# A transpose moved from TensorE to 32x32 blocks on VectorE, another seven-product scheme for q, k and v, and another order in the last first-stage group

## The chip, the cores and the metric

The kernel runs on one core of a Trainium2 chip. The metric is the time of one launch on the device, in microseconds (us); lower is better. The engines are named as the profile names them: PE is TensorE, DVE is VectorE, ACT is ScalarE, POOL is GpSimd and SP is SyncE, which here only issues transfers.

## The reference

Two graph layers over 4096 nodes with 512 features and one adjacency matrix (4096 x 4096, ones with probability 1/128). Each layer's result is added to its input and normalised over the features.

```python
# layer 0: four heads of 128
support = x @ weight                       # (N, 4, 128) by heads
w = leaky_relu(f1[None] + f2[:, None], 0.2)   # f1, f2: support times weight_u, weight_v
attn = softmax(where(adj, w, -1e30)) * adj
x = layernorm(x + attn @ support + bias + x @ proj_w + proj_b)
# layer 1: eight heads of 64
q, k, v = x @ Wqs, x @ Wks, x @ Wvs
scores = q @ k.T / 8 + 0.01 * eye - 1e16 * (1 - max(adj, eye))
x = layernorm(x + concat_heads(softmax(scores) @ v) @ Wo)
```

## The kernel before

The program is one long sequence, written out by hand: the order of the Python statements is the order of each engine's queue. Work that is due some steps later is put in a list with `later.at(n, fn)` and issued by `later.step()`. The rows are taken in 8 groups of 512 (`G`, `NG`) or in 32 tiles of 128 (`P`, `NT`).

**First products (L847, to about 210 us).** For each group g, `x @ weight` (kind "s") and `x @ proj_w` (kind "b") are each made as seven block products with shared sums instead of eight. A group is thus 14 products; the list `usual` alternates the kinds, `begin` (group 0) takes all "s" first, and `end` (group 7) is an order of its own. Products 2, 3 and 4 accumulate onto the PSUM buffers of 1, 5 and 7 after ScalarE or VectorE has taken those out (L864 to L875). `dots` (L818, VectorE) makes f1 and f2 from the finished blocks; `factors` takes the exponentials on ScalarE, scales the values on GpSimd (L700) and stores them from SP. The rows of x arrive so that 32x32 block transposes on VectorE (`turn_x`, L741) give the layout that the products need. Before the first product 14 dummy transposes run on TensorE (L887). `early` starts the first aggregation steps (`signs`, `front`) within group 7.

**Aggregation (L1077, 210 to 1136 us).** Four windows w of 1024 target rows, four heads h, 32 source tiles j: 512 steps. In a step VectorE makes the weights p (L641; every second step also a masked sign, L636) three steps ahead (`LA`), in four buffers, and TensorE multiplies them with the values. `beside_unit` issues transfers beside the steps; u counts the steps of a window. At the end of a window the eight tiles are closed beside the next window's steps: `close` takes statistics on VectorE (L511, L513), `normalise` runs on ScalarE (L1050) and stores the row block to `x1_d`. Some steps later `turn` transposes the tile with four TensorE transposes into PSUM (L1058), and `turned` copies it out on ScalarE (L1063) and stores it to `x1T_d`. `load_xT` brings it back for the next stage.

**q, k and v (L1193 and L1186, to about 1438 us).** Four pairs of groups; for each pair, k, q and v are made by `gemm` as seven block products each. `order` is the order of the products, `of_weights` and `of_features` say which sums (L1157, L1161) they need, and `beside` hangs other work behind a product. Products 4, 5 and 7 accumulate onto the buffers of 2, 3 and 1. ScalarE copies (L1200), VectorE adds or copies (L1239, L1246, L1254) and GpSimd adds (L1215) put the results together, and SP stores them (L1206, L1211). The closing of window 3 runs beside the first sets of this stage. Three score tiles of the last stage are made before the last v product.

**Attention (L1128 and L1390, to the end).** 1024 units of scores, exponentials, mask and products with v, then the output projection. The change does not touch it, except for the shape of `x1_d`.

Of the kernel before, what the change touches and what calls it, by code (L numbers as in the profile page):

```python
# [429 lines left out]
def tile_gat_then_masked_attention(  # L430
# [59 lines left out]
    x1_d = [dram.tile([P, D], F32, name=f"x1_d{i}") for i in range(NT)]  # L490
# [6 lines left out]
    x1T_d = [dram.tile([P, KC, G], F32, name=f"x1T_d{g}") for g in range(NG)]  # L497
# [43 lines left out]
    def wait_by_tile(name, bufs, **kw):  # L541
# [16 lines left out]
    order = (2, 3, 4, 5, 1, 6, 7)  # L558
    of_weights = {1: ((0, 0), (1, 1), ALU.add), 2: ((1, 0), (1, 1), ALU.add),
                  5: ((0, 0), (0, 1), ALU.add), 6: ((1, 0), (0, 0), ALU.subtract),  # L560
                  7: ((0, 1), (1, 1), ALU.subtract)}
    of_features = {1: ((0, 0), (1, 1), ALU.add), 3: ((0, 1), (1, 1), ALU.subtract),
                   4: ((1, 0), (0, 0), ALU.subtract), 6: ((0, 0), (0, 1), ALU.add),
                   7: ((1, 0), (1, 1), ALU.add)}
    plain_weights = {3: (0, 0), 4: (1, 1)}
    plain_features = {2: (0, 0), 5: (1, 1)}
# [3 lines left out]
    with tc.tile_pool(name="l0", bufs=NG) as l0, \  # L570
# [75 lines left out]
        with tc.tile_pool(name="l0s", bufs=2) as sp:  # L646
# [76 lines left out]
            for c in range(NCJ):  # L723
# [4 lines left out]
                if c < NCJ - 3:  # L728
                    for k in range(CJ):
# [3 lines left out]
            early = {3: lambda: signs(0, 0, 0), 5: lambda: front(0, 0, 0), 6: lambda: front(0, 0, 1),  # L733
                     7: lambda: signs(0, 0, 2), 10: lambda: front(0, 0, 2)}
# [151 lines left out]
            for _ in range(14):  # L886
                nc.tensor.transpose(warm[:, 0:P], ident, ident)  # L887
# [15 lines left out]
            for m in range(2):  # L903
# [6 lines left out]
            end = [("s", 1), ("b", 1), ("s", 5), ("s", 2), ("s", 6), ("s", 7), ("b", 5),  # L910
                   ("s", 3), ("b", 2), ("s", 4), ("b", 6), ("b", 7), ("b", 3), ("b", 4)]
            for g in range(NG):
# [7 lines left out]
                for k, (kind, i) in enumerate(plan):  # L920
# [35 lines left out]
        xTs = {}  # L956
# [13 lines left out]
        with wait_by_tile("l0v", 2) as vp:  # L970
            pools[1] = vp, vp

            def beside_unit(w, h, j):
# [30 lines left out]
                elif u % 4 == 0 and NT <= u < NT + 4 * KC:  # L1004
# [578 lines left out]
```

## Time and profile before

| what | value |
|---|---|
| median of 3 runs | 3356.52 us (3354.63 to 3357.25) |
| profiled execution | 3352.42 us, span 3350.6 us |
| granted TensorE clock, mean | 0.998 |
| PE busy | 3321.0 us, 99% |
| DVE busy | 2361.2 us, 70% |
| ACT busy | 1987.3 us, 59% |
| POOL busy | 2222.0 us, 66% |
| aggregation products, L1077 | 919.2 us |
| q, k, v products, L1193 and L1186 | 298 us together |
| transposes of the first layer's result, L1058 | 128, of 273 ns |

The profile is of one execution, whose own time stands beside its span. Busy time of an engine is the union of its instructions; a matmul overlaps the next one's start, so what one costs is read from the distance of the starts. A row of the waits names who waited, for whom, the total in us, how often, and the longest. A row of the timeline has the start and the length in us, the engine, the line of the program, the operation and the tiles written and read.

### The profile page before, as it was taken

Reading aid. Unit: us, or ns where it says so; the run is one execution under the profiler, and the core shown is the slowest. Engines: PE = TensorE matmul, PEld = TensorE weight load, DVE = VectorE, ACT = ScalarE, POOL = GpSimd, SP = SyncE. Lnnn points to the kernel's source line nnn. Section 1 sums busy time; section 2 is a strip of 40 time slices with the busy share of each in tenths; the row PEclk is TensorE's granted clock in tenths of the full one; section 3 lists DMA queues with packets and bytes.
Section 4 is the critical chain, followed back from the end, with each engine's and each line's share of the span. In section 5 each row is a group of like instructions: output and inputs, shape, how many; then the busy total and the mean of one; then the engine's idle time right before and its main releaser. Section 6 shows DMA issues by size and latency. Waiting matters only on the chain.

```text
span 3350.6 us, 66620 instructions
## 1 busy us (share of the span) xinstructions
PE 3321.0 (99%) x27064; PEld 1947.6 (58%) x27064; DVE 2361.2 (70%) x2894; ACT 1987.3 (59%) x2463; POOL 2222.0 (66%) x1588
## 2 busy tenths in 40 slices
PE   9999999999999999999999999999999999999998
PEld 7889999999999755633333333333333333333332
DVE  6689898898999611167766667666666666667676
ACT  1366977878776421255656656566565656656564
POOL 5631040040020365589999999999999999999996
PEclk9999999999999999999999999999999999999999
DMA  8978969589531443379889987889989889897984
GB/s 189 231 182 155 242 153 209 140 194 189 149 105 64 118 159 113 138 206 209 197 206 219 223 208 188 212 195 246 207 193 211 193 204 253 190 210 186 212 195 112
DMA packets 399054, 620.41 MB, mean 185 GB/s; under 512 B 166672, under 2 KB 247568, under 8 KB 397712
## 3 DMA queue, kind: packets, MB, share of 16 engines
q0 software_dynamic: 97520, 258.77, 42.5%
q1 hardware_dynamic: 299344, 354.26, 34.4%
q8 instruction: 215, 3.52, 0.4%
q10 hardware_dynamic: 1872, 3.02, 0.3%
q14 instruction: 103, 0.84, 0.1%
HBM read 315.87 MB, written 117.64 MB: 129 GB/s over the span
## 4 chain that ended last, share of the span: by engine, by line
PE 87%; POOL 2%; DMA 2%; issue 1%; DVE 1%; ACT 0%; POOLq 0%; ACTq 0%; DVEq 0%
PE o_ps L1077 27%; PE o_ps L1390 24%; PE s_ps L1128 24%; PE s_ps L1193 5%; PE s_ps L1454 3%; PE s_ps L1186 3%; POOL q_sum L1365 2%; DMA p<-p 1%; PE s_ps L1409 0%; PE x_ps L1058 0%; POOL p L1375 0%; DMA k_d<-v_sb 0%; DVE p L1522 0%; PE x_ps L1186 0%; POOL q_sum L1361 0%
## 5 line engine op out<-in xcount | busy, mean ns | idle before, releaser
L1365 POOL TENSOR_TENSOR q_sum<-q_sum,p 128x1024 f32<-128x1024 f32 x538 | 1375.5, 2557 | 65.4 <-DMA p<-p 41.8
L1345 DVE TENSOR_TENSOR p<-s_ps,adjT 128x1024 f32<-128x1024 f32 x896 | 1043.6, 1215 | 467.9 <-ACT s_ps L1342 433.6
L1342 ACT ACTIVATE s_ps<-s_ps 128x1024 f32<-128x1024 f32 x1021 | 967.3, 1006 | 596.3 <-PE s_ps L1128 596.1
L1128 PE MATMUL s_ps<-q_sb,k_sb 64*64 64x512 f32 x8192 | 943.0, 589 | 1.8 <-DVE p L1345 1.8
L1390 PE MATMUL o_ps<-p,v_sb 64*64 64x512 f32 x8192 | 943.6, 590 | 0.0
L1077 PE MATMUL o_ps<-sup_t,p 128*128 128x129 f32 x8192 | 919.2, 275 | 1.2 <-DVE p L641 1.2
L1077 PEld LDWEIGHTS o_ps<-sup_t,p 128*128 128x128 f32 x8192 | 916.9, 192 | 1.4 <-DVE p L641 1.3
L641 DVE SCALAR_TENSOR_TENSOR p<-fr_t,dj,az 128x1024 f32<-128x1024 f32 x512 | 653.9, 1286 | 80.7 <-PE o_ps L1077 52.5
L1128 PEld LDWEIGHTS s_ps<-q_sb,k_sb 64*64 64x64 f32 x8192 | 312.5, 133 | 568.3 <-issue 454.5
L1390 PEld LDWEIGHTS o_ps<-p,v_sb 64*64 64x64 f32 x8192 | 310.1, 133 | 570.8 <-issue 560.8
L625 ACT ACTIVATE z<-fr_t,f 128x1024 fp8e4<-128x1024 f32 x512 | 558.2, 1144 | 124.1 <-DVE az L636 123.7
L1375 POOL DMA_DIRECT2D p<-p x412 | 438.9, 1305 | 10.2 <-PE o_ps L1390 8.6
L1041 POOL DMA_DIRECT2D agg<-base_d x32 | 28.7, 1208 | 516.0 <-ACT agg L1027 515.8
L1345 DVE TENSOR_TENSOR p<-s_ps,md 128x1024 f32<-128x1024 f32 x128 | 150.7, 1216 | 67.7 <-ACT s_ps L1342 63.4
L588 POOL COPY seen<-token 128x1 f32<-128x1 f32 x24 | 12.4, 516 | 248.4 <-DVE token L586 248.4
L636 DVE TENSOR_TENSOR az<-adjT,z 128x512 int32<-128x512 int32 x256 | 175.5, 686 | 2.0 <-ACT z L625 1.3
L1200 ACT ACTIVATE sb<-s_ps 128x1024 f32<-128x1024 f32 x35 | 35.9, 1025 | 192.6 <-PE s_ps L1193 129.8
L601 ACT ACTIVATE adjT<-stage 128x1024 fp8e4<-128x1024 bf16 x128 | 130.6, 1051 | 4.6 <-DMA stage<-adj_d 4.6
L1215 POOL TENSOR_TENSOR sb<-sb,sb 128x1024 f32<-128x1024 f32 x36 | 84.9, 2373 | 71.8 <-ACT sb L1200 71.8
L1239 DVE COPY k_sb<-s_ps 128x1024 f32<-128x1024 f32 x12 | 14.7, 1224 | 141.8 <-PE s_ps L1193 91.8
L1454 PE MATMUL s_ps<-wo_sb,on 128*128 128x512 f32 x240 | 110.8, 604 | 0.0
L1424 ACT ACTIVATE r<-r_h 32x256 f32<-32x256 f32 x248 | 102.3, 412 | 2.9
(179 smaller groups left out, 2134.5 us busy)
## 6 DMA issues: line engine op xcount, KB each, us to landing
p<-p POOLq DMA_DIRECT2D x412, 512.0 KB, 9.0
k_sb<-k_d SPq DMA_DIRECT2D x128, 512.0 KB
v_sb<-v_d SPq DMA_DIRECT2D x128, 512.0 KB
adj_d<-in_adj_dram POOLq DMA_DIRECT2D x32, 1024.0 KB, 10.7
sup_t<-sup_d SPq DMA_DIRECT2D x120, 258.0 KB
fr_t<-fr_d SPq DMA_DIRECT2D x16, 1024.0 KB
adjT_d<-adjT SPq DMA_DIRECT2D x32, 512.0 KB
adjT<-adjT_d SPq DMA_DIRECT2D x32, 512.0 KB
```

Of the source, the lines that this page charges most:

```text
L625: nc.scalar.activation(z[:, k, :], fr_t[w, h][:, 0, :], AF.Sign, bias=fs[j // GT][:, 0, (j + k) % GT, h:h + 1], saturate=False)
L636: nc.vector.tensor_tensor(az.bitcast(I32), adjT[w, j // CJ][:, j % CJ:j % CJ + 2, :].bitcast(I32), z.bitcast(I32), op=ALU.bitwise_and)
L641: nc.vector.scalar_tensor_tensor(p, fr[:, 1, :], dj[j // GT][:, j % GT, h:h + 1], az_t[w, h, j // 2][:, j % 2, :], op0=ALU.max, op1=ALU.mult)
L1077: nc.tensor.matmul(o[t // BK][:, t % BK, :], p[:, t * P:(t + 1) * P], s, start=(j == 0 and t % BK == 0), stop=(j == NT - 1), skip_group_ch ...
L1128: nc.tensor.matmul(s[c:c + MS, e, :], k[r, a + c:a + c + MS], qt[g, m][r, :], start=True, stop=True)
L1193: nc.tensor.matmul(half, a[:, c, n * P:(n + 1) * P], x[:, c, :], start=not more and c == 0, stop=c == 1, skip_group_check=True)
L1342: nc.scalar.activation(s, s, AF.Exp)
L1345: nc.vector.tensor_tensor(p, s, keep[:, None, :].to_broadcast([P, HP, G]), op=ALU.mult)
L1365: nc.gpsimd.tensor_tensor(q, q, p, op=ALU.add)
L1375: later.at(2, lambda: nc.gpsimd.dma_start(a, b, accum_op=ALU.add))
L1390: nc.tensor.matmul(o[c, n, :], v[r, j % CH, c], p[r, e, :], start=(j == 0), stop=(j == NT - 1))
L1454: nc.tensor.matmul(s, on_t[g][:, m, t * P:(t + 1) * P], wo_sb[:, m, :], start=(m == 0), stop=(m == NP1 - 1))
```

## The change

First, the first layer's result is no longer transposed on TensorE. `x1_d` now holds one array per group; `load_x1` reads half a group (256 rows) in four transfers so that each quarter of the partitions holds another 128 features, and `turn_x1` transposes it with one VectorE block transpose for each quarter of the result. The weights are loaded with their rows permuted to match, in four transfers where one was before (`load_w`). For the first pair of groups this is done beside the last window's steps; for a later pair it hangs beside the k and q products of the pair before. Second, q, k and v use another scheme of seven products, whose sums build on one another (the scheme of the first products). Feature sums of the later pairs move from GpSimd to VectorE, and in place of four GpSimd sums per set there is one. Third, the last group of the first stage takes all "s" products and then all "b" products, with `factors` after the eleventh product, and `early` is moved accordingly. Fourth, 46 dummy transposes run at the start in place of 14.

```diff
-    x1_d = [dram.tile([P, D], F32, name=f"x1_d{i}") for i in range(NT)]
+    x1_d = [dram.tile([G, D], F32, name=f"x1_d{g}") for g in range(NG)]
...
-    x1T_d = [dram.tile([P, KC, G], F32, name=f"x1T_d{g}") for g in range(NG)]
...
-    order = (2, 3, 4, 5, 1, 6, 7)
-    of_weights = {1: ((0, 0), (1, 1), ALU.add), 2: ((1, 0), (1, 1), ALU.add),
-                  5: ((0, 0), (0, 1), ALU.add), 6: ((1, 0), (0, 0), ALU.subtract),
-                  7: ((0, 1), (1, 1), ALU.subtract)}
-    of_features = {1: ((0, 0), (1, 1), ALU.add), 3: ((0, 1), (1, 1), ALU.subtract),
-                   4: ((1, 0), (0, 0), ALU.subtract), 6: ((0, 0), (0, 1), ALU.add),
-                   7: ((1, 0), (1, 1), ALU.add)}
-    plain_weights = {3: (0, 0), 4: (1, 1)}
-    plain_features = {2: (0, 0), 5: (1, 1)}
+    order = (1, 5, 2, 6, 7, 3, 4)
+    of_weights = {5: ((1, 0), (1, 1), ALU.add), 6: (5, (0, 0), ALU.subtract),
+                  7: ((0, 0), (1, 0), ALU.subtract), 3: ((0, 1), 6, ALU.subtract)}
+    of_features = {5: ((0, 1), (0, 0), ALU.subtract), 6: ((1, 1), 5, ALU.subtract),
+                   7: ((1, 1), (0, 1), ALU.subtract), 4: ((1, 0), 6, ALU.subtract)}
+    plain_weights = {1: (0, 0), 2: (0, 1), 4: (1, 1), 7: (1, 0)}
+    plain_features = {1: (0, 0), 2: (1, 0), 3: (1, 1)}
...
-            early = {3: lambda: signs(0, 0, 0), 5: lambda: front(0, 0, 0), 6: lambda: front(0, 0, 1),
-                     7: lambda: signs(0, 0, 2), 10: lambda: front(0, 0, 2)}
+            early = {5: lambda: signs(0, 0, 0), 8: lambda: front(0, 0, 0), 9: lambda: front(0, 0, 1),
+                     7: lambda: signs(0, 0, 2), 11: lambda: front(0, 0, 2)}
...
-            for _ in range(14):
+            for _ in range(46):
...
-            end = [("s", 1), ("b", 1), ("s", 5), ("s", 2), ("s", 6), ("s", 7), ("b", 5),
-                   ("s", 3), ("b", 2), ("s", 4), ("b", 6), ("b", 7), ("b", 3), ("b", 4)]
+            end = [(kind, i) for kind in ("s", "b") for i in (1, 5, 2, 6, 7, 3, 4)]
...
+                    if g == NG - 1 and k == 10:
+                        factors(g, s4)
...
                 if g + 1 < NG:
                     later.at(1, lambda g=g, s4=s4: factors(g, s4))
-                else:
-                    factors(g, s4)
...
-        def load_w(dst, src, c):
-            nc.sync.dma_start(dst[:, c], src[:, c * P:(c + 1) * P, :].rearrange("h p k -> p h k"))
-
-        def load_xT(g, pool=turn_p):
-            xTs[g] = pool.tile([P, KC, G], F32, name="xT1", bufs=2)
-            nc.sync.dma_start(xTs[g], x1T_d[g])
...
+        def load_w(dst, src, c, a):
+            f = a * P + c * SQ
+            nc.sync.dma_start(dst[a * SQ:(a + 1) * SQ, c],
+                              src[:, f:f + SQ, :].rearrange("h p k -> p h k"))
+
+        def load_x1(g, n, pool=turn_p):
...
+            if n == 0:
+                xTs[g] = pool.tile([P, KC, G], F32, name="xT1", bufs=2)
+            ys[g, n] = turn_p.tile([P, HG // SQ, P], F32, name="y1_sb", bufs=2)
+            for a in range(NQ):
+                nc.sync.dma_start(
+                    ys[g, n][a * SQ:(a + 1) * SQ],
+                    x1_d[g][n * HG:(n + 1) * HG, a * P:(a + 1) * P].rearrange(
+                        "(b r) f -> r b f", r=SQ))
+
+        def turn_x1(g, n, c):
+            nc.vector.transpose(
+                xTs[g][:, c, n * HG:(n + 1) * HG].rearrange("p (b r) -> p b r", r=SQ),
+                ys[g, n][:, :, c * SQ:(c + 1) * SQ])
...
-                elif u % 4 == 0 and NT <= u < NT + 4 * KC:
-                    load_w(wk, wks, (u - NT) // 4)
-                elif u == NT + 4 * KC + 16:
+                elif NT <= u < NT + KC * NQ:
+                    load_w(wk, wks, (u - NT) // NQ, (u - NT) % NQ)
+                elif u == NT + KC * NQ + CJ:
                     nc.vector.tensor_tensor(wk_low, block(wk, 1, 0), block(wk, 1, 1), op=ALU.add)
-                elif h == H0 - 1 and j in (NT // 2, NT // 2 + CJ):
-                    load_xT((j - NT // 2) // CJ)
+                elif u >= 2 * NT and u % CJ == 0:
+                    k = (u - 2 * NT) // CJ
+                    if k % 3 == 0 and k < 12:
+                        load_x1(k // 6, k // 3 % 2)
+                if w + 1 == NW and u >= 2 * NT + 8 and (u - 2 * NT - 8) % 3 == 0:
+                    k = (u - 2 * NT - 8) // 3
+                    if k < 16:
+                        turn_x1(k // 8, k // 4 % 2, k % 4)
...
-                    nc.sync.dma_start(x1_d[i], y)
+                    nc.sync.dma_start(x1_d[i // GT][i % GT * P:(i % GT + 1) * P, :], y)
                 later.at(6, normalise)
-                later.at(8 if w + 1 < NW else 11, lambda: turn(y, i))
-
-            def turn(y, i):
-                p = xp.tile([P, KC, P], F32, name="x_ps")
-                for c in range(KC):
-                    nc.tensor.transpose(p[:, c, :], y[:, c * P:(c + 1) * P], ident)
-                later.at(2, lambda: turned(p, i))
-
-            def turned(p, i):
-                x1T = turn_p.tile([P, KC, P], F32, name="x1T", bufs=4)
-                nc.scalar.activation(x1T, p, AF.Copy)
-                nc.sync.dma_start(x1T_d[i // GT][:, :, i % GT * P:(i % GT + 1) * P], x1T)
...
             for dst, src in ((wq, wqs), (wv, wvs)):
                 for c in range(KC):
-                    load_w(dst, src, c)
+                    for a in range(NQ):
+                        load_w(dst, src, c, a)
...
-                sb = {i: sp.tile([P, 2 * G], F32, name=f"sb{i}", bufs=1) for i in (2, 3, 1)}
+                u2, p5 = (sp.tile([P, 2 * G], F32, name=n, bufs=2) for n in ("u2", "p5"))
...
+                def add(dst, t):
+                    n = 2 * G // len(t)
+                    for k, src in enumerate(t):
+                        part = slice(k * n, (k + 1) * n)
+                        nc.vector.tensor_tensor(dst[:, part], src, u2[:, part], op=ALU.add)
+
                 t = {}
                 for i in order:
-                    if i in (2, 3) or i == 6:
+                    if i in (1, 5, 6):
                         t[i] = new()
-                    elif i == 1:
+                    elif i == 7:
                         t[i] = [xp.tile([P, GT, P], F32, name="x_ps").rearrange(
                             "p t r -> p (t r)") for _ in range(2)] if last else new()
                     else:
-                        t[i] = t[{4: 2, 5: 3, 7: 1}[i]]
-                    if i == 7 and last:
+                        t[i] = t[{2: 1, 3: 5, 4: 7}[i]]
+                    if i == 4 and last:
                         for n in range(3):
                             first[n] = score(0, 0, n)
                             nc.scalar.activation(first[n], first[n], AF.Exp)
-                    product(i, t[i], more=i in (4, 5, 7))
-                    if i in sb:
-                        copy(sb[i], t[i])
-                    if i == 3:
-                        pool(sb[3], sb[3], sb[2], ALU.subtract)
-                    elif i == 4:
+                    product(i, t[i], more=i in (2, 3, 4))
+                    if i == 1:
+                        copy(u2, t[i])
+                    elif i == 5:
+                        copy(p5, t[i])
+                    elif i == 2:
+                        copy(out["11"], t[i])
+                        store("11")
+                    elif i == 6:
+                        add(u2, t[i])
+                    elif i == 7:
+                        add(out["22"], t[i])
+                        pool(out["22"], out["22"], p5, ALU.add)
+                        later.at(1, lambda: store("22"))
+                    elif i == 3:
+                        add(out["12"], t[i])
+                        store("12")
+                    elif last:
                         copy(out["21"], t[i])
+                        pool(out["21"], out["21"], u2, ALU.add)
+                        store("21", nc.gpsimd)
+                    else:
+                        add(out["21"], t[i])
                         store("21")
-                    elif i == 5:
-                        nc.vector.tensor_copy(out["12"], t[i][0])
-                        store("12")
-                        pool(sb[2], out["21"], out["12"], ALU.subtract)
-                    elif i == 1:
-                        pool(sb[1], sb[1], sb[3], ALU.add)
-                        pool(sb[2], sb[2], sb[3], ALU.add)
-                    elif i == 6:
-                        nc.vector.tensor_tensor(out["22"], t[i][0], sb[1], op=ALU.add)
-                        store("22")
-                    elif i == 7:
-                        if last:
-                            copy(out["11"], t[i])
-                            pool(out["11"], out["11"], sb[2], ALU.add)
-                            store("11", nc.gpsimd)
-                        else:
-                            nc.vector.tensor_tensor(out["11"], t[i][0], sb[2], op=ALU.add)
-                            store("11")
                     for fn in beside.get(i, []):
                         fn()
                     later.step()
 
             for pair in range(NG // 2):
-                if pair + 1 < NG // 2:
-                    for n in range(2):
-                        load_xT(2 * (pair + 1) + n, turn_p if pair % 2 else sp)
+                more = pair + 1 < NG // 2
+                halves = [(2 * pair + 2 + n // 2, n % 2) for n in range(4)] if more else []
+
+                def bring(n):
+                    load_x1(*halves[n], turn_p if pair % 2 else sp)
+
+                def turn(n):
+                    for c in range(KC):
+                        turn_x1(*halves[n], c)
+
                 beside = {}
                 if pair == 0:
-                    combine_features(nc.vector, 0, 3)
-                    combine_features(nc.vector, 0, 4)
-                    for i in (5, 1, 6, 7):
-                        todo = beside.setdefault(order[order.index(i) - 3], [])
-                        todo.append(lambda i=i: combine_weights(nc.vector, wk, wk_s, i))
-                        if i != 5:
-                            todo.append(lambda i=i: combine_features(nc.vector, 0, i))
-                    beside.setdefault(1, []).append(
+                    combine_features(nc.vector, 0, 5)
+                    for n, i in ((1, 6), (5, 7), (2, 3)):
+                        beside.setdefault(n, []).append(
+                            lambda i=i: combine_weights(nc.vector, wk, wk_s, i))
+                    for n, i in ((1, 6), (5, 7), (2, 4)):
+                        beside.setdefault(n, []).append(
+                            lambda i=i: combine_features(nc.vector, 0, i))
+                    beside.setdefault(6, []).append(
                         lambda: nc.scalar.activation(wq, wq, AF.Copy, scale=float(KD) ** -0.5))
-                    for i, n in ((2, 1), (5, 6), (1, 6), (6, 7), (7, 7)):
+                    for i, n in ((5, 7), (6, 7), (7, 3), (3, 4)):
                         beside.setdefault(n, []).append(
                             lambda i=i: combine_weights(nc.gpsimd, wq, wq_s, i))
+                if more:
+                    for k, n in ((1, 0), (5, 1)):
+                        beside.setdefault(k, []).append(lambda n=n: bring(n))
+                    for k, n in ((7, 0), (4, 1)):
+                        beside.setdefault(k, []).append(lambda n=n: turn(n))
                 gemm(wk, wk_s, "k", pair, beside)
                 beside = {}
                 if pair == 0:
-                    for i in (2, 5, 1, 6, 7):
-                        beside.setdefault(i, []).append(
+                    for i, n in ((5, 5), (6, 2), (7, 6), (3, 7)):
+                        beside.setdefault(n, []).append(
                             lambda i=i: combine_weights(nc.gpsimd, wv, wv_s, i))
-                if pair == NG // 2 - 1:
+                if more:
+                    for k, n in ((1, 2), (5, 3)):
+                        beside.setdefault(k, []).append(lambda n=n: bring(n))
+                    for k, n in ((7, 2), (4, 3)):
+                        beside.setdefault(k, []).append(lambda n=n: turn(n))
+                else:
                     for c in range(3):
                         load_adjT(0, c)
                     load_q(0, 0)
                 gemm(wq, wq_s, "q", pair, beside)
                 beside = {}
-                if pair + 1 < NG // 2:
-                    for i in of_features:
-                        beside.setdefault(i, []).append(
-                            lambda i=i: combine_features(nc.gpsimd, pair + 1, i))
+                if more:
+                    for i, n in ((5, 5), (6, 6), (7, 7), (4, 4)):
+                        beside.setdefault(n, []).append(
+                            lambda i=i: combine_features(nc.vector, pair + 1, i))
                 else:
-                    beside[2] = [lambda: load_kv(0, 0, 0)]
-                    beside[3] = [lambda: [load_adjT(0, c) for c in range(3, NCJ - 2)],
+                    beside[5] = [lambda: load_kv(0, 0, 0)]
+                    beside[2] = [lambda: [load_adjT(0, c) for c in range(3, NCJ - 2)],
                                  lambda: [finish_md(0, t) for t in range(GT)]]
-                    beside[6] = [lambda: load_kv(0, 0, 1),
+                    beside[7] = [lambda: load_kv(0, 0, 1),
                                  lambda: [load_adjT(0, c) for c in range(NCJ - 2, NCJ)]]
                 gemm(wv, wv_s, "v", pair, beside)
                 xTs.pop(2 * pair)
...
```

More of the change, by code (lines that the diff above doesn't have):

```diff
@@ L955, in tile_gat_then_masked_attention @@
         wk_low = turn_p.tile([P, KC // 2, D // 2], F32, name="wk_low", bufs=1)
-        xTs = {}
-        def load_w(dst, src, c):
-            nc.sync.dma_start(dst[:, c], src[:, c * P:(c + 1) * P, :].rearrange("h p k -> p h k"))
-        def load_xT(g, pool=turn_p):
-            xTs[g] = pool.tile([P, KC, G], F32, name="xT1", bufs=2)
-            nc.sync.dma_start(xTs[g], x1T_d[g])
+        ys, xTs = {}, {}
+        def load_w(dst, src, c, a):
[15 more added lines that the diff above has]
+                ys[g, n][:, :, c * SQ:(c + 1) * SQ])
         def block(w, m, c):
@@ L1138, in tile_gat_then_masked_attention @@
                 for c in range(KC):
-                    load_w(dst, src, c)
+                    for a in range(NQ):
+                        load_w(dst, src, c, a)
             def spare():
                 return lp.tile([P, 2, 2, D // 2], F32, name="adjT1", bufs=NCJ + 3)
-            wk_s, wq_s = ([spare() for _ in range(3)] for _ in range(2))
-            wk_s, wq_s = ({i: t[n // 2][:, n % 2] for n, i in enumerate(of_weights)}
-                          for t in (wk_s, wq_s))
+            wk_s, wq_s = [spare()], [spare() for _ in range(2)]
+            wk_s = {5: wk_low, 6: wk_s[0][:, 0], 3: wk_s[0][:, 1], 7: block(wk, 1, 0)}
+            wq_s = {5: wq_s[0][:, 0], 6: wq_s[0][:, 1], 3: wq_s[1][:, 0], 7: block(wq, 1, 0)}
+            wv_s = {i: sp.tile([P, 2, D // 2], F32, name=f"wv_s{i}", bufs=1) for i in (5, 6, 3)}
+            wv_s[7] = block(wv, 1, 0)
             x_s = {i: spare().rearrange("p a b r -> p (a b r)").rearrange(
-                "p (c r) -> p c r", c=2) for i in (3, 4, 1, 6, 7)}
-            wv_s = {i: sp.tile([P, 2, D // 2], F32, name=f"wv_s{i}", bufs=1)
-                    for i in of_weights}
-            wk_s[2] = wk_low
+                "p (c r) -> p c r", c=2) for i in of_features}
             def features(pair, c, n):
@@ L1156, in combine_weights @@
                 a, c, op = of_weights[i]
-                engine.tensor_tensor(sums[i], block(w, *a), block(w, *c), op=op)
+                a, c = (sums[k] if isinstance(k, int) else block(w, *k) for k in (a, c))
+                engine.tensor_tensor(sums[i], a, c, op=op)
             def combine_features(engine, pair, i):
                 a, c, op = of_features[i]
-                engine.tensor_tensor(x_s[i], features(pair, *a), features(pair, *c), op=op)
+                a, c = (x_s[k] if isinstance(k, int) else features(pair, *k) for k in (a, c))
+                engine.tensor_tensor(x_s[i], a, c, op=op)
             def take_out(name):
@@ L1169, in gemm @@
                 out = {}
-                for n, c in enumerate(("21", "12", "22", "11")):
+                for n, c in enumerate(("11", "22", "12", "21")):
                     out[c] = take_out("k_sb" if n % 2 else "v_sb")
-                sb = {i: sp.tile([P, 2 * G], F32, name=f"sb{i}", bufs=1) for i in (2, 3, 1)}
+                u2, p5 = (sp.tile([P, 2 * G], F32, name=n, bufs=2) for n in ("u2", "p5"))
                 def new():
@@ L1458, in load_y @@
                 y_t[g, t] = wp.tile([P, D], F32, name="y1", bufs=5)
-                nc.sync.dma_start(y_t[g, t], x1_d[g * GT + t])
+                nc.sync.dma_start(y_t[g, t], x1_d[g][t * P:(t + 1) * P, :])
             def close1(g, t, s, wait=4):
```

## Prediction

> **What bounds the kernel now.** I read the page's busy line first, then the waits of TensorE, its groups by form, and its timeline where first-layer results are closed.
>
> ```profile
> PE 3321.0 (99%) x27064; PEld 1947.6 (58%) x27064; DVE 2361.2 (70%) x2894; ACT 1987.3 (59%) x2463; POOL 2222.0 (66%) x1588
> ```
>
> TensorE is busy for all but 29.6 us of 3350.6. A microsecond of its work that goes is a microsecond saved, provided that no other engine falls behind; everything that only moves work between the other engines is worth nothing while TensorE is fed. Its few waits:
>
> ```profile
> PE o_ps L847 <- DVE xT L741: 4.1, 1, 4.1
> PE o_ps L847 <- DVE base L870: 3.2, 2, 2.8
> ...
> PE o_ps L1077 <- DVE p L641: 1.2, 1, 1.2
> ...
> PE s_ps L1193 <- POOL adjT L1157: 0.7, 1, 0.7
> ```
>
> They lie at the start (8.7 us), at the seam from the first products to the aggregation (207.8 and 218.1), and at the first q product (1162.6). The work to be removed, by form:
>
> ```profile
> L1058 PE MATMUL x_ps<-ident,agg 128*128 128x128 f32 x128 | 19.2, 273 | 0.0
> ```
>
> 273 ns is the duration of one and 19.2 us their union with overlaps. What one displaces is read from starts in the timeline:
>
> ```profile
> 476.35 3.74 PE L1077 MATMUL o_ps<-sup_t,p 128*128 128x129 f32 x32
> 479.92 0.60 PE L1058 MATMUL x_ps<-ident,agg 128*128 128x128 f32 x4
> 480.36 1.95 PE L1077 MATMUL o_ps<-sup_t,p 128*128 128x129 f32 x16
> 482.14 0.60 PE L1058 MATMUL x_ps<-ident,agg 128*128 128x128 f32 x4
> 482.58 3.74 PE L1077 MATMUL o_ps<-sup_t,p 128*128 128x129 f32 x32
> ```
>
> Two aggregation steps take 3.57 us (1.785 each); the four transposes of a tile push the next start back by 0.44 us. VectorE in the same stretch:
>
> ```profile
> 480.57 0.69 DVE L511 BATCH_NORM_STATS2 bn_st<-agg 128x6 f32<-128x512 f32 x1
> 481.37 0.18 DVE L513 BATCH_NORM_AGGREGATE bn_mv<-bn_st 128x2 f32<-128x6 f32 x1
> 481.47 0.69 DVE L636 TENSOR_TENSOR az<-adjT,z 128x512 int32<-128x512 int32 x1
> ...
> 482.26 2.48 DVE L641 SCALAR_TENSOR_TENSOR p<-fr_t,dj,az 128x1024 f32<-128x1024 f32 x2
> ```
>
> It never waits there: 36.94 us busy in 458 to 497.
>
> **What the Trainium skill says.** "VectorE: DVE Perf Modes", The three transpose paths: VectorE transposes inside 32x32 blocks only. The trace agrees in that the existing transposes (L741) serve here only since the loads spread the rows over blocks; a 128x256 one takes 401 ns, and four start within 1.42 us, 0.355 apart. "TensorE: Matmul & The Clock Gate", PE-mode transpose: its output goes to PSUM and needs a copy afterwards. The trace shows that copy (ACT L1063, 0.58 us), which goes too. The same page, What's actually happening: TensorE runs at half clock until it has been busy for a window of some 3.4 us. The trace agrees: clock 0.51 in 8.4 to 11.8 us, after an idle 4.1 us. "GPSIMD Engine Reference", Specifications: GpSimd shares its SBUF interfaces with VectorE instructions of two SBUF inputs. Here two p steps that take 2.48 us alone took 3.19 at 194.85, while GpSimd added.
>
> **The parts and their costs.**
>
> *Transposes off TensorE.* 32 tiles x 0.44 us = 14.1 us removed: 24 tiles in the closing stretches of windows 0 to 2 (10.6), 8 in the q/k/v stage (3.5). The pitch there is the same (1179.91 to 1180.35).
>
> *What is late next.* In a closing stretch VectorE does eight pairs of normalisation statistics, some 0.80 us each, on top of 1.62 us per step (1.28 for p, half of 0.69 for the mask). It normally completes p 2.9 us ahead (p 14 at 461.8, used at 464.7) and regains about 0.15 us per step. The tightest is p 24: done at 483.5 (half of the last row above), used at 484.37, so 0.9 us are left. Four tiles' transposes precede it. Without them step 24 wants to start at 484.37 - 4 x 0.44 = 482.61, so TensorE waits 0.9 us. The other windows show the same pattern (715.7 against 714.8; 947.9 against 947.0). Cost 3 x 0.9 = 2.7 us. Bounds: 0, and 10.6 (all that was freed there).
>
> *Block transposes in window 3.* Sixteen of 0.36 us over 48 steps, 0.24 per two steps, beside a VectorE that waits 0.30 us for TensorE every two steps. Hidden; behind them queues p, with its 2.9 us lead. If the cover were gone, 5.7 us; below nothing is excluded, as TensorE waits for nothing there. I take 0. Their loads (SP, four of 128 KB per half) are issued some 8 steps (14 us) ahead; the nearest row, 256 KB of agg<-base_d, lands after 6.3 us.
>
> *q, k, v.* Still seven products of 3.44 us, so TensorE's work is equal. Per product set VectorE goes from three evacuations to four (4 x 1.22 = 4.9 us), plus eight block transposes (2.9) in k and q, or four feature sums (4 x 1.2) in v: at most 9.7 of 24.1 us. GpSimd drops from four sums of 2.35 us to one, and its five feature sums per pair go; ScalarE loses a copy. Hidden by 14 us of idle VectorE; without that cover 1 to 5 us per set. Product 2 adds onto the buffer of product 1 after a 1.02 us copy with product 5 (3.44) between, product 4 onto that of 7 with product 3 between: no wait. The q set's first product now takes an unsummed weight block, so the 0.7 us wait for L1157 goes. In the last v set the second early score needs the buffer of product 3, whose add (1.22 + 0.2) starts when only one score (0.9) lies between: + 0.5 us. Net -0.2, bounds -0.7 and +1.5.
>
> *Queues.* SP issues 64 block loads and 36 more weight loads, less 32 stores and 8 loads: + 60 of 0.4 to 0.7 us. wk's sixteen queue around a 3 MB load that ends by 975 and are used about 995. wq and wv (32 issues from 1127) end by 1149, and wq is scaled at about 1150, while TensorE needs it at 1161.7. ScalarE and VectorE work queued behind those waits is not due before then. Taken as 0; at worst 3.
>
> *Last group by kind.* VectorE ran without a pause from 191.26 (the sum after product 6) to p 4 at 217.9, and TensorE waited for it at 207.78 and 218.07. Ordered by kind, product 6 starts at 187.53 in place of 189.26, so this queue starts 1.73 us earlier with the same contents (both bias sums stay on VectorE). One gap of 0.5 us opens (product 3 ends at 192.9). Against that, GpSimd's value sums, which stretched VectorE's rows there by some 3.7 us, fall earlier, beside PSUM reads. b 4 then starts at about 204.8 without its wait, step 0 at 206.5, and step 4 follows p 4. Gain 1.3 to 3.7; I take 2.3, with 0 and 4 as bounds. Moving the factors to k = 10 puts two reductions and a small transpose (0.4 us) ahead of two adds: counted. GpSimd's sums, SP's four stores of values and four row stores come earlier; nothing in the first pass needs them before step 28.
>
> *Warm-up.* 32 more transposes. At the cold pitch (0.215) until the clock rises at about 5.0, then 0.11, they end at about 8.3, before xT at 8.67. Product 1 then runs at full clock and ends at 10.5 in place of 12.2. But its copy cannot start: ScalarE issues loads until 11.24 and loads a table until 12.54. So 0. Bounds: -1, and + 2.6 if the clock stayed low (46 x 0.215 + 3.56 ends at 14.8).
>
> Sum: -14.1 + 2.7 - 0.2 - 2.3 = -13.9 us. The profiled execution took 3352.4 us (span 3350.6), giving 3338.5; it lies 4.1 below the median of 3356.5, and against that the forecast is 3342.6.
>
> **Rivals.**
>
> *VectorE becomes the bound in the closing stretches.* For it: 95% busy there. Against: its lead is not used up before p 24. If all 10.6 us come back as waits for p, -3.5 - 0.2 - 2.3 = -6.0: 3350.5, no measurable difference.
>
> *The block loads land late (slower).* VectorE works in order, so a block transpose that waits for its load holds back the adds that free PSUM, and TensorE stops at the next product. Place: twelve half-loads in the q/k/v stage, rows of 512 bytes, the first behind 32 weight loads. Each is issued four or five products ahead (13.8 us or more), and 3.4 us more pass before the buffer is wanted. To end 6.7 us slower it takes 20.6 us of stalls, 1.7 per half: landing after 18.9 us, three times the 6.3 of the nearest row. Price at 20 us each: 12 x 2.8 = 33.6, so 3376.
>
> *The seam gives nothing and the start loses.* If contention moves with the sums and the clock stays low: -13.9 + 2.3 + 2.6 = -9.0: 3347.5. This is also the case that the reordering and warm-up don't do what they say.
>
> **How the numbers follow.** A measurement of this kernel tells about 0.2% (6.7 us) from no change. Forecast, gains of 10 to 18: 0.62. Seam and start lost, or more waits in closing, gains of 6.7 to 10: 0.17. VectorE bound: 0.11. Late loads: 0.10. Faster 0.79, same 0.11, slower 0.10. The range is 3336 (seam at 4, no closing waits: -13.9 - 1.7 - 2.7 = -18.3, and run to run 2) to 3351 (the VectorE case); beyond lie the late loads and half of that case.
>
> **What would show it.** No L1058 and no L1063; about 0.9 us of TensorE waits for p L641 in each of the three closing stretches; SP landing without VectorE waits on y1_sb; step 0 near 206.5; TensorE busy near 3307. Many TensorE waits behind transposes waiting for a DMA in 1140 to 1430, or a q/k/v stage longer than 298 us, would make it wrong.

## The result, and the profile after

The changed kernel takes 3376.6 us (median of 7 runs) where the kernel before takes 3353.9 beside it: a ratio of 1.0069, 95% interval 1.0058 to 1.0080. It is slower by some 23 us; forecast was a gain of 14. One of the seven executions took 9023 us, which nothing here explains; it is left out of the ratio. The other six lie between 3367.8 and 3388.6, a spread of 21 us where the seven of the kernel before have 4.8: what costs the time does not cost the same in each execution. The profiled execution took 3376.4 us.

The page's busy line of the kernel after:

```profile
PE 3320.9 (98%) x26968; PEld 1945.3 (58%) x26968; DVE 2402.3 (71%) x2981; ACT 1957.6 (58%) x2418; POOL 2098.6 (62%) x1535
```

TensorE issues 96 transposes less on balance (128 gone, 32 more in the warm-up) and yet is as long busy as before, and the span is 24 us longer. The waits of the kernel after (who waits for whom: us in total, times, longest):

```profile
ACT adjT L598 <- DMA stage<-adj_d: 60.4, 9, 12.1
PE o_ps L1083 <- DVE p L638: 25.5, 12, 5.0
PE s_ps L1201 <- POOL bn_nb L518: 4.8, 1, 4.8
PE o_ps L844 <- ACT z L861: 3.3, 1, 3.3
```

The last row lies at the start, at the second product. (Line numbers moved: p L641 is now L638, the aggregation L1077 is L1083, q/k/v L1193 is L1201.) The first row was 4.6 us before, the second 1.2. Where the time sits shows when the aggregation is cut into its 16 passes of 32 steps (four to a window, the very last left out), from the starts of its products. The last column is the time from the first product of the q/k/v stage to the first product with v in the stage behind it:

| us | window 0 | window 1 | window 2 | window 3 | q/k/v stage |
|---|---|---|---|---|---|
| before | 58.6, 57.2, 57.2, 57.2 | 60.7, 57.2, 57.2, 57.2 | 60.7, 57.2, 57.2, 57.2 | 60.7, 57.2, 57.2 | 299.2 |
| after | 58.8, 57.2, 57.2, 57.2 | 58.3, **61.3, 70.7**, 57.2 | 58.3, **62.7, 65.1**, 57.2 | 58.2, 57.2, 57.2 | 302.0 |

The first pass of each window, in which the tiles are closed, gained what was forecast. What was not forecast are 31 us in the passes behind it, in windows 1 and 2 alone. Some 22 us of it are waiting (25.5 in TensorE's row for p, less 3.7 that are left in version e5 below); the rest is TensorE at a lower clock after the waits (0.91 in 560 to 616 us, 1.00 in the 350 us ahead of that). One such stop in the timeline, on three engines:

```profile
808.92 2.00 ACT L598 ACTIVATE adjT<-stage 128x1024 fp8e4<-128x1024 bf16 x2 [5.79 <-DMA stage<-adj_d]
813.04 0.69 DVE L633 TENSOR_TENSOR az<-adjT,z 128x512 int32<-128x512 int32 x1 [3.44 <-ACT z L622]
815.17 6.19 PE L1083 MATMUL o_ps<-sup_t,p 128*128 128x129 f32 x53 [1.28 <-DVE p L638]
```

ScalarE takes its instructions in the order of its queue. It stops at the shrink (L598), since the data for it have not come. The shrink makes the next window's adjacency ready and is not urgent; the signs z queued behind it are, and the wait runs on through VectorE to TensorE.

The data come in two transfers. `narrow` (issued by GpSimd, L586; L589 before) rewrites 1 MB of the adjacency into `adj_d`; some steps later `turn_in0` (issued by SP, L592; L595 before) brings it in as a DMA transpose. The rows of both, taken by tile between 430 and 900 us (in the first line how long SP's queue was held by one transpose, as ns min/median/max; the second line is the narrowing transfer). Before:

```profile
L595 SPq DMA_TRANSPOSE stage<-adj_d x16: 4060/8276/14874, 512.5 to 860.5; - x16
DMA to landing us min/median/max: 8.5/13.3/23.5
```

After:

```profile
L592 SPq DMA_TRANSPOSE stage<-adj_d x16: 4042/8086/26212, 501.0 to 886.0; - x16
DMA to landing us min/median/max: 8.7/23.3/32.7
```

Neither was changed. The longest transpose took 26 us in place of 15, and the narrowing 23 in place of 13 in the median: they run at the same time. The DMA queues of the kernel after in such a stretch (757 to 783 us; packets, MB, share of 16 engines' time; q1 has SP's transfers, q0 GpSimd's):

```profile
q1 hardware_dynamic: 3990, 1.11, 82.8%
q0 software_dynamic: 1756, 1.76, 49.3%
```

82.8% of 16 x 26 us over 3990 packets is 86 ns a packet (the two shares add up to more than 100%, so packets of one queue overlap with those of the other, and the time of a packet holds waiting). Version e5 below has a transpose nearly alone (770 to 775 us):

```profile
q1 hardware_dynamic: 4128, 1.05, 95.4%
q0 software_dynamic: 26, 0.03, 15.3%
```

That is 18 ns a packet. The Trainium skill ("DMA: Bandwidth & Descriptors", Queues, rings and completion order) says that each DMA engine takes turns between the queues that have work for it, and sends a whole packet of one before it turns to the next. The traces agree in that SP's small packets suffer beside GpSimd's larger ones, by 4.7 times; that the turns are the reason is not shown, as a packet of the page holds several descriptors and need not be a packet of the profile. The same page (Rules for kernel authors), in a row on transfers that corrupt each other's data, says "A transpose next to ordinary DMAs needs nothing"; of time it does not speak, and time is what was lost here.

Why do they meet now? SP's queue in the closing of window 1 and 2 has the stores of the closed tiles, then the next values and factors, then the transposes. Window 2 before:

```profile
728.69 2.24 SPq L616 DMA_DIRECT2D fr_t<-fr_d  x1
731.02 13.17 SPq L988 DMA_DIRECT2D sup_t<-sup_d  x8
744.53 36.18 SPq L595 DMA_TRANSPOSE stage<-adj_d  x3
```

and after:

```profile
740.21 0.37 SPq L613 DMA_DIRECT2D fr_t<-fr_d  x1
740.68 8.18 SPq L1000 DMA_DIRECT2D sup_t<-sup_d  x8
749.56 69.04 SPq L592 DMA_TRANSPOSE stage<-adj_d  x3
```

From the start of the window (671.9 and 685.5) the transposes are issued at 72.6 before and at 64.0 after: SP gets through sooner without the x1T stores and what paced them (e2, e6 and e7 below). The narrowing is paced by VectorE's steps and hardly moved (its fourth transfer is issued at 69.9 and 68.7). By the packets' own times the first transpose starts 3.6 us after the fourth narrowing transfer before, and 1.9 us ahead of it after.

The second loss is at the start of the q set. The chain of work that ended last in 1140 to 1200 us, in order of time, names it from end to end:

```profile
1159.39 9.24 DMA wo_sb<-in_L_gnn_Wo_dram
1168.64 0.31 SPq L956
...
1169.60 7.60 DMA wq<-in_L_gnn_Wqs_dram
...
1183.98 0.46 SPq L967
...
1185.46 3.21 DMA y_sb<-x_d
...
1188.80 1.49 DVE xT L973 x4
```

and the timeline its price (TensorE's rows, and one of VectorE's):

```profile
1184.02 3.60 PE L1201 MATMUL s_ps<-xT,wq 128*128 128x512 f32 x8
1191.06 1.23 DVE L1229 TENSOR_TENSOR v_sb<-s_ps,u 128x1024 f32<-128x1024 f32 x1
1192.43 5.88 PE L1201 MATMUL s_ps<-adjT,adjT 128*128 128x512 f32 x8 [4.82 <-POOL bn_nb L518]
1198.15 3.60 PE L1201 MATMUL s_ps<-xT,wq 128*128 128x512 f32 x8
```

The ninth of 32 weight loads waits for `wo_sb`'s load from another engine to land, the block loads (y_sb, L967) follow the last of the 32, VectorE waits 10.2 us for them at its first block transposes, and TensorE stops for 4.8 us; its next product takes 2.3 us longer at the lower clock (0.61 in 1192.4 to 1198.2): 7.1 in all. The row names GpSimd's bn_nb, which this product doesn't read. VectorE's add behind the block transposes (L1229), which frees a PSUM buffer, ended at 1192.29: 0.14 us ahead of the product.

### The profile page after: what moved, and what is told of

It is laid out like the page before. It is cut to its first block, busy times and chain, and to the rows that moved or that the text cites. A ratio compares the mean times of both kernels' runs of the same rounds, so it can differ in the third digit from the quotient of the medians.

```text
span 3374.5 us, 66468 instructions
## 1 busy us (share of the span) xinstructions
PE 3320.9 (98%) x26968; PEld 1945.3 (58%) x26968; DVE 2402.3 (71%) x2981; ACT 1957.6 (58%) x2418; POOL 2098.6 (62%) x1535
## 4 chain that ended last, share of the span: by engine, by line
PE 71%; DMA 3%; DVE 1%; SPq 1%; ACT 0%; issue 0%; POOL 0%; POOLq 0%; DVEq 0%; ACTq 0%
PE o_ps L1419 26%; PE s_ps L1134 26%; PE o_ps L1083 8%; PE s_ps L1201 5%; PE s_ps L1483 3%; PE s_ps L1194 3%; DMA stage<-adj_d 2%; SPq L592 1%; PE s_ps L1438 1%; DVE p L638 0%; DMA p<-p 0%; DMA wo_sb<-in_L_gnn_Wo_dram 0%; DMA sup_t<-sup_d 0%; DVE p L1551 0%; DVE bn_st L510 0%; DMA wq<-in_L_gnn_Wqs_dram 0%
## 5 line engine op out<-in xcount | busy, mean ns | idle before, releaser
L1083 PE MATMUL o_ps<-sup_t,p 128*128 128x129 f32 x8192 | 924.8, 276 | 26.3 <-DVE p L638 25.5
L1083 PEld LDWEIGHTS o_ps<-sup_t,p 128*128 128x128 f32 x8192 | 922.0, 193 | 29.1 <-DVE p L638 28.1
L638 DVE SCALAR_TENSOR_TENSOR p<-fr_t,dj,az 128x1024 f32<-128x1024 f32 x512 | 648.3, 1284 | 59.6 <-PE o_ps L1083 32.5
L1404 POOL DMA_DIRECT2D p<-p x412 | 436.8, 1296 | 10.2 <-PE o_ps L1419 9.3
L1374 DVE TENSOR_TENSOR p<-s_ps,md 128x1024 f32<-128x1024 f32 x128 | 150.7, 1217 | 68.7 <-ACT s_ps L1371 64.5
L598 ACT ACTIVATE adjT<-stage 128x1024 fp8e4<-128x1024 bf16 x128 | 130.5, 1050 | 60.4 <-DMA stage<-adj_d 60.4
L1223 POOL TENSOR_TENSOR k_sb<-k_sb,p 128x1024 f32<-128x1024 f32 x12 | 30.8, 2564 | 196.7 <-DVE k_sb L1229 190.2
L1208 ACT ACTIVATE u<-s_ps 128x1024 f32<-128x1024 f32 x12 | 12.3, 1024 | 167.6 <-PE s_ps L1201 104.4
L1229 DVE TENSOR_TENSOR u<-s_ps,u 128x1024 f32<-128x1024 f32 x12 | 14.7, 1225 | 111.6 <-PE s_ps L1201 81.8
```

The source lines that it names most:

```text
L638: nc.vector.scalar_tensor_tensor(p, fr[:, 1, :], dj[j // GT][:, j % GT, h:h + 1], az_t[w, h, j // 2][:, j % 2, :], op0=ALU.max, op1=ALU.mult)
L1083: nc.tensor.matmul(o[t // BK][:, t % BK, :], p[:, t * P:(t + 1) * P], s, start=(j == 0 and t % BK == 0), stop=(j == NT - 1), skip_group_ch ...
L1374: nc.vector.tensor_tensor(p, s, keep[:, None, :].to_broadcast([P, HP, G]), op=ALU.mult)
L1404: later.at(2, lambda: nc.gpsimd.dma_start(a, b, accum_op=ALU.add))
```

## The experiments

Times are medians of the runs; the kernel before had 3354.5 to 3355.1 beside them. Waits and passes are those of the one profiled execution of each version.

**e1: the narrowing half a period earlier.**

```diff
-                        if u == (16 + 8 * c if w else 22 + 7 * c):
+                        if u == (12 + 8 * c if w else 22 + 7 * c):
```

> The changed kernel, with the transfers that narrow the next window's adjacency (windows 1 to 3) started four steps, 7.1 us or half of their period, earlier; the tokens on VectorE that release them move along. Nothing on TensorE changes. Theory A (collision: the DMA transposes of the next window's adjacency run while these transfers run, each slows the other, ScalarE waits at the shrink L598, and TensorE behind it): the transposes of window 3 sum to about 60 us in place of 94, ScalarE's waits at L598 for the stage fall from 60 us to under 10, the second and third passes of windows 1 and 2 go back to 57.2 us (from 61.3, 70.7, 62.7 and 65.1), and the time falls by about 31 us to 3343 to 3350. Rival B (VectorE's closing work is what delays p, whatever the transfers do): the passes stay above 61 us and the time stays at 3368 to 3389. Rival C (the SP queue is too full with the block loads of weights): as B, since the SP queue is unchanged.

3348.6 us, 0.9980 of before (0.9971 to 0.9989). All passes of windows 1 and 2 are 58.3 or 57.2, and ScalarE no longer waits for the stage there (one wait of 2.1 us is left, in window 0, whose narrowing was not moved). The twelve runs lie within 6.0 us of each other. By tile:

```profile
L592 SPq DMA_TRANSPOSE stage<-adj_d x16: 3883/4248/14689, 501.8 to 854.2; - x16
DMA to landing us min/median/max: 8.1/10.4/13.9
```

Both medians are now below those of the kernel before. Nothing was moved but the narrowing and VectorE's small token that releases it, so the collision is shown to be the cause of the 31 us (28.0 between the medians). The q/k/v stage kept its 302.1.

**e2: the traffic of the stores alone.** After the store of the row block:

```diff
+                if w + 1 < NW:
+                    later.at(10, lambda: nc.sync.dma_start(
+                        again_d[i // GT][:, :, i % GT * P:(i % GT + 1) * P],
+                        y.rearrange("p (c r) -> p c r", c=KC)))
```

> The changed kernel plus one store of each closed tile of windows 0 to 2 from SP, in pieces of 512 bytes, to an array that nothing reads. It brings back the traffic of the transposed store that the change took out, not the TensorE transposes. Theory A with its trigger (without these stores the transposes start some 5 us earlier against the narrowing transfers, and fall on top of them): the transposes of windows 2 and 3 go back to some 62 us each, the stalls of 31 us vanish, and the time is 3343 to 3350 although there is more to store. Rival: if the trigger is something else (the time that TensorE gained in the closing, or the added weight loads), more traffic changes nothing or makes it worse: 3368 to 3395.

3372.7 us (four runs, 3367.8 to 3387.7): the rival was right that this isn't enough. ScalarE's wait for the stage fell only to 37.2 us, from 60.4.

**e3: the kernel before with its narrowing half a period later** (20 + 8 * c in the same line).

> The kernel before, with the narrowing transfers of windows 1 to 3 started four steps (7.1 us, half of their period) later, nothing else. Theory A: the DMA transposes of the kernel before run between these transfers by luck of phase; shifted, they overlap for most of their length, the transposes of windows 2 and 3 sum to over 85 us each (62 and 59 now), ScalarE waits at the shrink for tens of us, and the kernel is slower than before by 10 to 35 us without any part of the change. Rival: if the stalls of the changed kernel come from its own new work, this stays within 4 us of 3354.

The median, 3357.0 us, would by itself fit the rival. But the 20 runs lie between 3352.4 and 3383.8, 8 of them above 3364, where the kernel before spans 3351.7 to 3358.4. The profiled one (3376.3) has a pass of 76.9 us in window 2 and none in window 1. So the kernel before has the same trap, and a shift in time alone sets it off; it is entered in some executions only, which I had not expected.

**e4: the load of wo_sb placed in the text behind the 32 weight loads.**

> The changed kernel, with the load of the output weights (wo_sb, from ScalarE's queue) placed in the program after the 32 loads of wq and wv. Theory: a transfer waits for the one eight places before it in the program, and so the ninth load of wq waits 14.5 us for wo_sb, and 11 us pass with an idle SP queue; moved, SP's wait for wo_sb goes, ScalarE's wait of 7.4 us before the scaling of wq goes, and with it TensorE's wait of 4.8 us at the third q product. The time falls by about 5 us (less than one run tells). Rival (GpSimd's own work, the statistics of the closing, delays the sum of wq): the 4.8 us stay.

A single run: 3390.4 us, SP's wait 15.6 and TensorE's 5.0 us. Neither went; the longer total is the collision again, which cost 43 us in the passes of this execution. The load's place in the text was not the place that it got among the transfers: by the trace it still increments the semaphore (100) that the ninth weight load waits for and increments next. The test needs a load that comes later in time.

**e5: e1, and wo_sb loaded at the second pair of groups.**

```diff
-        nc.scalar.dma_start(wo_sb, wo.rearrange("(c a) k e -> (a k) c e", a=HP))
...
+                if pair == 1:
+                    nc.scalar.dma_start(wo_sb, wo.rearrange("(c a) k e -> (a k) c e", a=HP))
```

> The changed kernel with the narrowing transfers of windows 1 to 3 four steps earlier, and with the load of the output weights (wo_sb) issued at the start of the second pair of groups in the q/k/v stage, after all loads of wq and wv have landed. Moving that load behind the weight loads in the text of the program left SP's wait of 15 us as it was, since both became ready at the same place; here it cannot come between them. Theory (the ninth load of wq waits for wo_sb's to land, the scaling of wq, the sums on GpSimd and the first block transposes on VectorE are late by that, and TensorE stops 4.9 us and then runs its next product 2.3 us slower at a lower clock): SP's wait for wo_sb goes, the q set has no wait and all its products take 3.60 us, the q/k/v stage falls from 302.1 to about 295 us, and the time from 3348.6 by 7 to 3338 to 3345. Rival (the 32 weight loads themselves are what is late: GpSimd's and VectorE's waits stay): the stage stays at 302 us and the time at 3346 to 3351.

3341.1 us, 0.9960 of before (0.9946 to 0.9973): faster than both kernels. The stage takes 294.7 us, and the product that stopped runs without a wait:

```profile
1154.56 3.60 PE L1200 MATMUL s_ps<-xT,wq 128*128 128x512 f32 x8
1157.99 3.60 PE L1200 MATMUL s_ps<-adjT,adjT 128*128 128x512 f32 x8
1161.42 3.60 PE L1200 MATMUL s_ps<-xT,wq 128*128 128x512 f32 x8
```

VectorE still waits for the first block load, 2.8 us, at no cost. In the aggregation of e5 four waits for p are left, one at step 3 (1.2 us) and one in each of the three closings:

```profile
PE o_ps L1083 <- DVE p L638: 3.7, 4, 1.2
```

**e6 and e7: the old work of the closing back, with and without its stores.**

```diff
+                if w + 1 < NW:
+                    later.at(8, lambda: turn(y, i))
...
+                for c in range(KC):
+                    nc.tensor.transpose(p[:, c, :], y[:, c * P:(c + 1) * P], ident)
+                later.at(2, lambda: turned(p, i))
...
+                nc.scalar.activation(x1T, p, AF.Copy)
+                nc.sync.dma_start(x1T_d[i // GT][:, :, i % GT * P:(i % GT + 1) * P], x1T)
```

The last line is in e6 only.

> The changed kernel with the old transposes of windows 0 to 2 back beside the new ones: four TensorE transposes of each closed tile, ScalarE's copy of them, and the store from SP to an array that nothing reads. It asks whether the phase of the transposes against the narrowing transfers came from this work at all. If so: no stalls, window 3's transposes sum to some 60 us, and the time is that of the changed kernel less 31 us of stalls, plus 24 x 0.44 - 2.6 = 8 us of transposes that it does anew: about 3348 to 3358. If the phase came from elsewhere (the weight loads, the earlier start): stalls as in the changed kernel, 3375 to 3395.

> As the one before, but without its stores: TensorE's transposes and ScalarE's copies only. The stores alone (3372.7 us) left most stalls. If the pace of TensorE and ScalarE in the closing is what matters, the stalls are gone here as well and the time is 3348 to 3358; if it takes both the stores and the pace, they stay, 3370 to 3395.

e6: 3356.6 us, aggregation 928.3 us as before (928.0), and no pass with a stall; one of its 20 runs took 3366.6, the others at most 3360.4. e7: 3374.2 us with a pass of 75.2. Together with e2 this shows the trigger: the stores and the work that paces them, not either alone. The start of the first DMA transpose of window 3's adjacency, and of the fourth narrowing transfer, in us from the start of window 2 (first packet in the trace; the sum is over the 8 transposes of that window, each from its first packet to the end of its last):

| kernel | transpose | narrowing | sum of 8 transposes | wait of ScalarE for the stage, whole run |
|---|---|---|---|---|
| before | 76.9 | 73.3 | 59.0 | 4.6 |
| after | 71.1 | 73.0 | 94.3 | 60.4 |
| e2, stores only | 72.8 | 73.3 | 83.1 | 37.2 |
| e7, TensorE and ScalarE only | 70.7 | 74.5 | 98.9 | 30.6 |
| e6, all of it | 77.2 | 73.3 | 62.8 | 9.2 |
| e1, narrowing earlier | 68.7 | 64.8 | 45.6 | 2.1 |

Where the narrowing is under way first, each transpose loses some microseconds and the pairs stay apart; where the transpose is first, both grow until they overlap the next pair. The stores and the copies which pace them hold SP back by 5.8 us only together. In e3 the two windows began alike within 0.1 us, with the third narrowing transfer 5 us ahead of the first transpose, and only one of them collided: the order is not the whole condition, and its edge stays open.

**e8: the third part undone on top of e5** (the old `end`, `early`, and factors after the group).

> The version with earlier narrowing and the late load of wo_sb, with the third part of the change undone: the last first-stage group in its old order, the old places of the first aggregation steps in it, and factors after the group. Expected from the traces, in which the stretch from the second product to step 4 of the aggregation is 204.9 us before and 200.0 after: step 4 comes about 4.8 us later, with waits for base and p of some 3 us again, and the whole is 4 to 5 us slower than that version (3342 to 3350). By the sum of the prediction it would be 2.3 us. If the seam gained nothing, within 1 us.

3342.4 us against 3341.1: within the scatter of single runs. The traces are finer: from the third product to step 0 it is 194.6 us before, 191.5 after, 192.5 in e5, and 194.6 again in e8, which has its wait back:

```profile
PE o_ps L844 <- DVE base L867: 3.2, 2, 2.8
```

So the seam gives 2 to 3 us. The 4.8 of the expectation was a slip: the wait for p that stood at step 4 before stands at step 3 after, and the two were compared.

**e9: 14 dummy transposes on top of e5.**

> The version with earlier narrowing and the late load of wo_sb (3341.1 us), with 14 dummy transposes at the start in place of 46, the fourth part of the change undone. The prediction took the warm-up for 0 (bounds -1 and +2.6), since ScalarE's copy sets the second product. In the traces the second product begins at 13.20 in the kernel before and at 13.9 to 14.5 in all versions with 46, and ScalarE's copy before it at 12.55 against 13.3 to 13.8. If the 46 transposes are the cause of that, the second product is back near 13.2, the first one takes 3.56 us in place of 1.99, and the time falls by about 1 us, which the runs can hardly tell. If it is only the landing of the first loads, which has nothing to do with TensorE, the second product stays at 13.9 or later and the time within 1 us.

3342.4 us, the second product at 13.67. The kernel before had it at 13.20 in its profiled execution, but e10, with 14 too, at 14.24: the start varies with something else, probably the landing of the first loads (in e10 TensorE waits 4.7 us there for w_sb), and the warm-up does nothing measurable.

**e10: the two moves of e5 in the kernel before.**

> The kernel before with the same two moves: narrowing four steps earlier, and wo_sb loaded at the start of the second pair of groups. Theory: both moves only undo side effects of the change, and the gain of 13 us of the version with them is the change's own. The kernel before has no stalls of the kind, and its SP wait for wo_sb holds back a load (xT) that nobody needs soon: 3351 to 3357, no difference. Rival: the moves are worth something by themselves, and part of the 13 us is theirs: below 3350.

3358.8 us, 1.0011 of before (1.0005 to 1.0018): a little slower than was expected, with one of 21 runs at 3368.7, which is unexplained. The moves are no gain of their own; here the q set's wait for L1156 even grew from 0.7 to 3.4 us. So the 13.4 us by which e5 beats the kernel before are the change's, not theirs.

## Why the prediction was wrong

With both side effects undone the changed kernel takes 3341.1 us; forecast were 3342.6. The other terms of the sum were right, and one that stood in it as 0 was wrong by some 36 us (3376.6 less 3341.1; 31 and 7 in the traces). That the terms add up is not luck: closing passes, q/k/v stage and seam gave 7.0, 4.5 and 2.1 us in e5's trace (whose last stage, which the change leaves alone, was 2.2 us longer than before).

- *Transposes off TensorE, and what is late next*: right. Each closing pass went from 60.7 to 58.3 us (-2.4; forecast -3.5 + 0.9 = -2.6), and the wait stands where it was put. The timeline of the kernel after:

```profile
482.01 2.16 PE L1083 MATMUL o_ps<-sup_t,p 128*128 128x129 f32 x17 [0.85 <-DVE p L638]
729.45 1.72 PE L1083 MATMUL o_ps<-sup_t,p 128*128 128x129 f32 x13 [0.85 <-DVE p L638]
972.70 1.50 PE L1083 MATMUL o_ps<-sup_t,p 128*128 128x129 f32 x11 [0.80 <-DVE p L638]
```

- *Block transposes in window 3*: right, its passes are unchanged at 57.2.
- *q, k and v*: right but for its loads. In e5 the stage is 4.5 us shorter (forecast 3.5 + 0.2).
- *Seam*: forecast 2.3, measured 2 to 3. Step 0 is at 207.7, not 206.5, for the third product began 1.2 us late.
- *Warm-up*: right at 0. It counts as busy time, though (4 us more before step 0), which the sign "TensorE busy near 3307" left out; e5 has 3312.3.
- *Queues: this is the step that failed* ("Taken as 0; at worst 3"), in two places. First, it counted the issues that SP gains and loses, and took the 32 stores that go as relief. It did not ask what stands behind them in SP's queue. Those are DMA transposes of another window, whose time against GpSimd's transfers the stores and the work that paced them had set: 31 us. No rival had it; even the case of late loads looked only at loads that the change brings. Second, "wq and wv (32 issues from 1127) end by 1149" rested on 32 x 0.7 us of issue. In the trace of after they take from 1149.4 to 1184.0, 34.6 us in place of the 22, of which SP waits 14.5 us for wo_sb. The same wait was in the trace of before, 11.5 us ahead of the load of xT, where nobody needed it. With wo_sb out of the way the 32 take 25.3 us.
- *The slower rival* (block loads late, VectorE holding back TensorE) named the mechanism of the second loss, but it came at one half-load of the twelve and cost 7 us, not 33.6. That its price, 3376, is nearly the time measured is chance. The 0.10 on the slower side thus held a smaller cause than the one that decided.

Open are the exact condition of the collision (e3), and why a transpose and an ordinary transfer slow each other by more than their added packets: in the medians of e1 the one takes 4.2 us and the other 10.4, and in the kernel after the narrowing alone takes 23.3.

## What to carry to other kernels

A transfer that is removed changes the phase of everything behind it in its queue, that is, the time at which it meets the other transfers: list what the queue issues next, and what runs on the other queues at that time. Where two background streams are both far from urgent, give them different times on purpose rather than leave it to luck; half a period was worth 28 us here. When one transfer is split into many, look for the waits that SP already has in that place, since a wait that hid behind one early load will stand in front of most of the pieces.

## What the runs showed of the hardware

- A DMA transpose of 1 MB took 4.2 us in the median where it was mostly kept apart from GpSimd's 1 MB transfers (e1), and up to 26.2 where it ran beside one (after). Those transfers grew from 10.4 us to 23.3 in the median, and to 32.7 at most.
- In this program transfers from SP and ScalarE use one set of eight semaphores in turn (100 to 107 in the trace), so a load on one queue can wait for a load on the other that it has nothing to do with: 14.5 us here.
- After a wait of 4.8 us a q product took 5.88 us in place of 3.60, at a mean clock of 0.61: the slower product cost about half as much again as the wait itself.
